# A two-layer graph network on one core: work reordered at both ends of the program

## The chip, the core and the metric

The kernel runs on one core of a Trainium2 chip. Five engines work side by side, each in the order of its own queue: TensorE (PE) multiplies matrices, VectorE (DVE), ScalarE (ACT) and GpSimd (POOL) work elementwise, and SyncE (SP) issues most of the transfers (DMAs). They wait for each other on semaphores. The metric is the time of one execution on the device, in microseconds (us); lower is better.

## The reference

There are 32 items of 512 nodes with 512 features, one 512 x 512 adjacency matrix, and two layers. The first is masked attention of 8 heads of 64 features, the second a graph convolution with a symmetrically normalized adjacency; each adds its input and normalizes.

```python
def _L0_gnn_ref(x, adj, Wq, bq, Wk, bk, Wv, bv):
    q = (x @ Wq + bq).reshape(b, n, H, HD)          # k, v likewise; H = 8, HD = 64
    scores = jnp.einsum('bihd,bjhd->bhij', q, k) / jnp.sqrt(jnp.float32(HD))
    scores = scores + jnp.where(adj == 0, -1e9, 0.0)[None, None, :, :]
    out = jnp.einsum('bhij,bjhd->bihd', jax.nn.softmax(scores, axis=-1), v)
    return out.reshape(b, n, H * HD)

def _L1_gnn_ref(x, adj, weight, bias):
    d = jnp.where(adj.sum(axis=1) > 0, jax.lax.rsqrt(adj.sum(axis=1)), 0.0)
    norm_adj = adj * d[:, None] * d[None, :]
    return jnp.einsum('nm,bmo->bno', norm_adj, jnp.einsum('bni,io->bno', x, weight)) + bias

x = _layernorm(x + _L0_gnn_ref(x, adj, Wq, bq, Wk, bk, Wv, bv))
x = _layernorm(x + _L1_gnn_ref(x, adj, weight, bias))
```

## The kernel before

**Order.** The program is written out by hand. Small helper functions return lists of pieces, a piece being one product and what follows it; `run`, `weave` and `cut` put the lists in an order, and the wrapper `InOrder` pins every engine to the order in which the program names its instructions. That wrapper records each instruction, so all of them show as line 44 in the profile, and they are told apart by their tiles. `unshifted` is the fast way through; it counts conditions under which its arithmetic is not good enough in `bad`, and `general` would run only if `bad` were positive.

**Products in seven parts.** The 512-wide products with the weights are made of seven half-size products instead of eight, so the operands need combinations: a tile of seven slots holds four quarters (0 to 3), and slots 4, 5, 6 and then 2 are made by subtracting or adding slots. `combine` does that for the transposed x (tile `XT`, in the profile xT), `weigh` for the weights `wv`, `wk`, `wq`, `w1`. `seven` yields the seven pieces k = 0 to 6 in the slot order (0,0), (1,1), (5,5), (6,6), (4,4), (3,2), (2,3). Each piece writes one PSUM tile of the pool `ps_mm`, which has three buffers (tile mm), and VectorE or ScalarE takes it from there into running sums e1, u2 and the results.

**Start.** The first x is not transposed by VectorE but turned by PE: `turn_first(j, i)` multiplies with the identity into an mm tile and copies that into XT[:, 2j+i], VectorE for i = 0, ScalarE for i = 1. In the queues, `weigh(wv)` and `weigh(wk)` stand on POOL, `values_of(0)` (value products; `middle` forms u2 and adds the value bias bv_r to it on POOL), then `keys_and_queries(0, 0)` and `(0, 1)` with the adjacency between them. `adjacency` writes the mask, and the adjacency twice: adjT in the rounded type that the convolution uses, and plainT unrounded. `compare(m)` later tests one quarter of the two for differences (a comparison that writes plainT and a reduction into `lost`).

**Middle.** `blocks` has four blocks of two heads for each item. In each block PE makes scores twice (pool ps_sc, two buffers, tile sc), VectorE clips and masks them (e<-sc,maskT), ScalarE exponentiates, POOL sums the exponentials (acc) and PE multiplies them with the values (av). Between these, `shares` deals out the products for the next item and the convolution of the one before. During item 0 the side work is a dictionary `beside`, keyed by the place of a piece in the list of products for item 1; all four `compare` stand behind pieces 10 and 12 there.

**End.** For item 31 (b = B - 1) there is nothing left to run beside. `finish` has `add_pair` (attention output and residual), `measure`, `root` (on POOL, the reciprocal root), `norm` (writes x1 and its rounded part HI, tile hi), `low` (the remainder, tile lo), `lift` (adds the layer's bias b1_r on POOL), `grow` and `judge` (three small checks on VectorE). `convolve` has `block(m)` (eight products with adjT into two sc tiles), `unload` and `parts` (the result into XT and its combinations), `second` (the seven products with w1), `extend` (POOL adds or subtracts), `measure`, `root` and `store`. For item 30, the pieces k = 4, 5, 6 of `second` are copied by ScalarE to tiles called side and summed by `extend(4)` to `extend(6)`. In the last lines `c` is the convolution of item 30 with its pieces `s`, `e` that of item 31, and `end` is `finish(31)`.

Of the kernel before, what the change touches and what calls it, by code (L numbers as in the profile page):

```python
# [17 lines left out]
P = 128  # L18
# [31 lines left out]
def unshifted(  # L50
# [29 lines left out]
    B, N, D = x.shape  # L80
# [4 lines left out]
    tensor, vector, scalar, gpsimd = (InOrder(tc, e) for e in (nc.tensor, nc.vector, nc.scalar, nc.gpsimd))  # L85
# [15 lines left out]
    HALF = N // 2  # L101
    X = {}
    XT = consts.tile([P, 7, 2, HALF], F32, name="xT")
# [14 lines left out]
    def turn(b, j):  # L118
# [4 lines left out]
        if j == 0 and b > 1:  # L123
            load_x(b, 1)

    def turn_first(j, i):

        p = ps_mm.tile([P, 2, HALF], F32, name="mm")
        for n in range(2):
            for u in range(2):  # L130
                for q in range(4):
                    at = q * P + (2 * i + u) * 32
                    tensor.matmul(
                        p[32 * q : 32 * (q + 1), u, ts(n, P)], R[0][2 * j + n][:, at : at + 32], ident,
                        start=True, stop=True,
                    )
        (scalar.copy if i else vector.tensor_copy)(XT[:, 2 * j + i], p)

    def combine(b, at):
        to, a, c = ((4, 2, 0), (5, 3, 4), (6, 3, 2), (2, 5, 1))[at]  # L140
        engine = gpsimd if b else vector
        engine.tensor_tensor(XT[:, to], XT[:, a], XT[:, c], ALU.subtract)
# [34 lines left out]
    def weigh(t, engine):  # L177
        for at in range(4):
            weigh_part(t, engine, at)
# [15 lines left out]
    for i in range(2):  # L195
# [3 lines left out]
        if i == 0:  # L199
            bv_r = load_row(bv, "bv_r", nc.scalar)  # L200
    wk = load_parts(Wk, "wk", nc.sync)
# [11 lines left out]
    b1_r = load_row(b1, "b1_r", nc.sync)  # L213
# [101 lines left out]
    def values_of(b):  # L315


        def multiply(p, i, j):
            for r in range(2):
                for u in range(2):  # L320
                    tensor.matmul(
                        p[:, r, :], XT[:, j, u, ts(r, P)], wv[:, i, u, :],
                        start=u == 0, stop=u == 1,
                    )

        def first(e1, p):
            V[b] = acts.tile([P, NT, D], F32, name="v")
            vector.tensor_add(e1, p, bv_r[:, None, :HALF].to_broadcast([P, 2, HALF]))

        def middle(u2, u1, p):  # L330
            vector.tensor_add(u2, u1, p)
            gpsimd.tensor_add(u2, u2, bv_r[:, None, HALF:].to_broadcast([P, 2, HALF]))

        def out(i, j):
            return V[b][:, 2 * j : 2 * j + 2, ts(i, HALF)]

        return seven(multiply, first, middle, out)
# [33 lines left out]
    E, ACC, AV, SM, YT, HI, LO = {}, {}, {}, {}, {}, {}, {}  # L371
# [126 lines left out]
    def finish(b):  # L498
# [96 lines left out]
            )  # L595

        def lift(i):
            gpsimd.tensor_add(YT[b][:, i, :], YT[b][:, i, :], b1_r)

        def grow(i):  # L600
            x1 = YT[b][:, i, :]
# [5 lines left out]
        def behind(f):  # L607
# [6 lines left out]
            pairs=[[(0, add_pair, (i, g)) for i in range(NT)] for g in ORDER],  # L614
            halves=[(0, root, (0, 2)), (0, root, (2, 2))],
# [156 lines left out]
    def run(pieces):  # L772
        for _, f, args in pieces:
            f(*args)
# [21 lines left out]
    put_off = [(0, more, ())]  # L796
# [2 lines left out]
    blocks = [(b, g) for b in range(B) for g in ORDER]  # L799
    S = len(blocks)  # L800
    weigh(wv, gpsimd)
    weigh(wk, gpsimd)
    first = values_of(0)
    turn_first(0, 0)
    turn_first(0, 1)
# [1 line left out]
    value_biases()  # L807
    turn_first(1, 0)
    turn_first(1, 1)
    combine(0, 0)  # L810
    combine(0, 1)
    run(first[1:2])
    combine(0, 2)
    combine(0, 3)
    scalar.activation(wq[:, :4], wq[:, :4], AF.Copy, scale=SCALE)
    run(first[2:])
    biases()
    wq_parts = [(0, weigh_part, (wq, vector, k)) for k in range(4)]
    first = keys_and_queries(0, 0)
# [6 lines left out]
    for k in range(S + 1):  # L826
        b, at = divmod(k, G)
        if at == 1:
            if 1 < b < B - 1:
                load_residual(b - 1)  # L830
            if b + 2 < B:
                load_x(b + 2, 0)
            if b + 1 < B:
                main, kq = keys_and_queries(b + 1, 0), keys_and_queries(b + 1, 1)
                if b:
                    main = values_of(b + 1) + main
                turn0, turn1 = turns(b + 2) if b + 2 < B else ([], [])
                main += kq[:5]
            if b == 0:
                w1_parts = [(0, weigh_part, (w1, gpsimd, i)) for i in range(4)]  # L840
                exact = [(0, compare, (m,)) for m in range(NT)]
                main += kq[5:]
                beside = {
                    2: put_off, 3: [(0, degrees, ())] + put_off, 6: put_off, 7: w1_parts[:1] + put_off,
                    8: w1_parts[1:2], 9: turn0 + w1_parts[2:3], 10: put_off + exact[:2], 11: put_off + w1_parts[3:],
                    12: exact[2:], 13: turn1,
                }
                side = early[5:6] + put_off + early[6:] + put_off
                side += sum(([piece] + beside.get(i, []) for i, piece in enumerate(main)), [])
                shares = cut(side, (4, 4, 4, 4))  # L850
            elif b < B - 1:
                f, c = finish(b - 1), convolve(b - 1)
                norm, low, grow, measure = f["norm"], f["low"], f["grow"], f["measure"]


                beside = {
                    0: rest[:1], 1: rest[1:3], 3: rest[3:4] + put_off, 4: rest[4:5],
                    5: rest[5:6] + f["inverse"] + put_off, 6: rest[6:] + f["scale"][:2], 7: f["scale"][2:] + f["add"],
                    8: measure[:2] + put_off, 9: measure[2:], 10: f["root"] + put_off, 11: norm[:1],
                    12: norm[1:2] + low[:1], 13: norm[2:3] + low[1:2], 14: norm[3:] + low[2:3],  # L860
                    15: low[3:] + f["lift"], 16: put_off + grow[:2], 17: put_off + grow[2:], 18: turn0 + f["judge"],
                }
                side = sum(([piece] + beside.get(i, []) for i, piece in enumerate(main)), [])
                side += c["first"] + c["parts"] + kq[5:] + turn1[:1]
                s = c["second"]
                if b < B - 2:
                    side += put_off + s[:1] + put_off + s[1:3] + turn1[1:2] + s[3:4] + turn1[2:3] + s[4:5]
                    side += turn1[3:4] + s[5:6] + c["measure"][:1] + turn1[4:] + s[6:] + c["measure"][1:2]
                    rest = c["measure"][2:] + c["root"] + c["store"]
                    shares = cut(side, (8, 8, 8, 8))  # L870
                else:
                    held, h, last = c, s, finish(b)
                    scale, add = last["scale"], last["add"]
                    side += h[:1] + last["inverse"] + h[1:2] + scale[:2] + h[2:3] + scale[2:] + add
                    shares = cut(side, (8, 8, 8, 4))
            else:
                f, c, last = last, convolve(b - 1), finish(b)
                s, first, low, lift, pairs = c["second"], c["first"], f["low"], f["lift"], last["pairs"]
                within = low[:1]
                shares = [  # L880
                    h[3:4] + f["measure"] + f["root"] + h[6:] + f["norm"] + f["judge"],
                    h[4:5] + low[1:3] + h[5:6] + low[3:] + lift + put_off + put_off + last["early"] + first[:2]
                    + held["measure"][:2] + first[2:3] + held["measure"][2:] + first[3:] + c["parts"] + f["grow"],
                    held["root"] + s[:2] + pairs[0] + pairs[1],
                    [],
                ]
# [40 lines left out]
    norm, low, lift, block, pairs, extend = end["norm"], end["low"], end["lift"], e["block"], end["pairs"], c["extend"]  # L927
    run(end["late"][:1] + pairs[2] + end["late"][1:] + s[2:3] + held["store"])
    run(sum((pairs[3][i : i + 1] + end["measure"][i : i + 1] for i in (0, 1)), []) + end["halves"][:1] + s[3:5])
    run(sum((pairs[3][i : i + 1] + end["measure"][i : i + 1] for i in (2, 3)), []) + extend[:1] + end["halves"][1:])  # L930
    run(s[5:6] + norm[:2] + low[:1] + block[:1] + low[1:2] + block[1:2] + lift[:1] + extend[1:2] + norm[2:] + low[2:3])
    run(block[2:3] + low[3:] + lift[1:2] + block[3:] + lift[2:] + end["judge"])

# [8 lines left out]
    vector.tensor_add(count, count, more)  # L944
    vector.memset(ones, 1.0)

    run(e["unload"] + e["parts"] + s[6:] + end["grow"] + extend[2:] + c["measure"][:2])
    s, tail, halves = e["second"], c["measure"][2:] + c["root"] + c["store"], e["halves"]
    run(s[:2] + halves[0] + s[2:3] + tail[:1] + s[3:4] + tail[1:3] + s[4:5])
    p = ps_mm.tile([1, 1], F32, name="mm")  # L950
    tensor.matmul(p, count, ones, start=True, stop=True)
    vector.tensor_scalar(bad, p, -1.0, float(P * B * NT * H + N), op0=ALU.mult, op1=ALU.add)
    run(tail[3:] + s[6:] + e["measure"][2:] + e["roots"][1:] + e["stores"][2:] + s[5:6] + halves[1] + e["roots"][:1])
    run(e["stores"][:2])
    return nc.values_load(bad, min_val=0, max_val=P * B * NT * H + N * N + N)

# [281 lines left out]
```

## Time and profile before

| | |
|---|---|
| time, median of 3 runs | 2820.21 us (2820.18 to 2822.76) |
| the profiled execution | 2821.64 us; span of the profile 2819.7 us |
| granted TensorE clock | 0.997 |
| TensorE busy | 2792.0 us, 99% of the span |
| VectorE, GpSimd, ScalarE busy | 2177.5, 1786.4, 1050.1 us |
| one POOL operation of two inputs, 128x512 | 1.28 us (yT<-yT,b_r, mean of 124) |
| one VectorE operation on PSUM and SBUF, 128x512 | 0.69 us (kq<-u,mm, mean of 128) |
| five value products (40 matmuls) in a row, from 16.07 | 8.87 us |

A profile is of one execution. Times of rows are from the span's start. Of a row "14.36 1.58" the first number is its start and the second its duration; consecutive rows of one engine overlap by about 0.1 us. A wait is idle time of an engine, put down to the instruction that ended it. The chain follows the last instruction back through what released it; "issue" in it is time for which the profile shows no releaser.

### The profile page before, as it was taken

To read this page: it belongs to the slowest core of one execution; us is meant where nothing else is said; L and a number is where in the kernel's file an instruction comes from. 1 tells how busy PE (TensorE), PEld (TensorE's weight loads), DVE (VectorE), ACT (ScalarE), POOL (GpSimd) and SP (SyncE) were. 2 spreads that over 40 slices of the span, in tenths; PEclk is the share of its full clock that TensorE was granted. 3 is DMA by queue.
4 is the path that set the end of the run, shared out by engine and by line. 5 is a ranking of instruction groups with operands and counts; after the bars stand their busy time and mean duration, and the time that the engine had idled before them with its cause. 6 is when DMAs were issued, how large, how long until landed. Compare 5 with 4: busy or idle time off the path is not lost.

```text
span 2819.7 us, 34592 instructions
## 1 busy us (share of the span) xinstructions
PE 2792.0 (99%) x12540; PEld 1874.8 (66%) x12540; DVE 2177.5 (77%) x3201; ACT 1050.1 (37%) x1323; POOL 1786.4 (63%) x1174
## 2 busy tenths in 40 slices
PE   8999999999999999999999999999999999999997
PEld 6566666666666666666666666666666666666655
DVE  5877877788777787777787778877777777778777
ACT  2333333343333433334333334333343333443343
POOL 3666665666666666666666666666666666666656
PEclk9999999999999999999999999999999999999999
DMA  4111121112221122221112211222112122112211
GB/s 120 32 29 49 49 59 43 43 48 52 57 57 42 38 52 54 57 45 42 49 49 60 53 42 37 53 56 57 42 41 53 49 56 46 42 49 49 60 38 50
DMA packets 379107, 141.04 MB, mean 50 GB/s; under 512 B 277808, under 2 KB 345392, under 8 KB 378928
## 3 DMA queue, kind: packets, MB, share of 16 engines
q1 hardware_dynamic: 377776, 137.17, 20.4%
q8 instruction: 101, 1.65, 0.2%
q10 hardware_dynamic: 1152, 1.57, 0.2%
q14 instruction: 78, 0.64, 0.1%
HBM read 71.83 MB, written 33.55 MB: 37 GB/s over the span
## 4 chain that ended last, share of the span: by engine, by line
PE 97%; DVE 2%; POOL 0%; issue 0%; DMA 0%; ACT 0%; POOLq 0%; DVEq 0%; ACTq 0%
PE mm L44 64%; PE sc L44 17%; PE av L44 16%; DVE e L44 1%; DVE xT L44 0%; DVE plainT L44 0%; POOL xT L44 0%; POOL acc L44 0%; DVE st L44 0%; DVE y L44 0%; DMA xr<-in_x_dram 0%; DVE lo L44 0%; DVE kq L44 0%; DVE lost L44 0%; DVE ve L44 0%
## 5 line engine op out<-in xcount | busy, mean ns | idle before, releaser
L44 ACT ACTIVATE e<-e 128x1024 f32<-128x1024 f32 x512 | 540.9, 1057 | 1075.8 <-DVE e L44 1059.2
L44 POOL TENSOR_TENSOR acc<-acc,e 128x1024 f32<-128x1024 f32 x248 | 587.5, 2369 | 94.3 <-ACT e L44 87.1
L44 DVE SCALAR_TENSOR_TENSOR e<-sc,maskT 128x1024 f32<-128x1024 f32 x512 | 597.9, 1208 | 22.1 <-PE sc L44 21.9
L44 PE MATMUL sc<-kq 64*128 64x512 f32 x2048 | 510.1, 616 | 3.6 <-DVE e L44 3.5
L44 PE MATMUL mm<-xT,wk 128*128 128x256 f32 x1792 | 469.7, 384 | 2.4 <-issue 2.0
L44 PE MATMUL av<-e,v 128*64 128x512 f32 x2048 | 467.9, 598 | 0.0
L44 PE MATMUL mm<-xT,wq 128*128 128x256 f32 x1792 | 459.9, 379 | 0.0
L44 PEld LDWEIGHTS mm<-xT,wk 128*128 128x128 f32 x1792 | 332.2, 190 | 115.9 <-issue 72.9
L44 PE MATMUL mm<-wv,xT 128*128 128x256 f32 x1792 | 405.3, 383 | 1.8 <-DVE xT L44 1.3
L44 PEld LDWEIGHTS mm<-wv,xT 128*128 128x128 f32 x1792 | 336.3, 191 | 72.7 <-issue 25.3
L44 POOL TENSOR_TENSOR acc<-e 128x1024 f32<-128x1024 f32 x126 | 297.2, 2359 | 134.3 <-ACT e L44 134.3
L44 PEld LDWEIGHTS mm<-xT,wq 128*128 128x128 f32 x1792 | 340.5, 190 | 46.3
L44 PEld LDWEIGHTS sc<-kq 64*128 64x128 f32 x2048 | 175.9, 186 | 271.4 <-issue 203.1
L44 PEld LDWEIGHTS av<-e,v 128*64 128x64 f32 x2048 | 135.5, 136 | 316.2 <-issue 293.4
L44 POOL TENSOR_TENSOR yT<-yT,b_r 128x512 f32<-128x512 f32 x124 | 154.6, 1279 | 167.7 <-DVE lo L44 167.7
L44 DVE TENSOR_TENSOR kq<-u,mm 128x512 f32<-128x512 f32 x128 | 88.0, 688 | 221.9 <-PE mm L44 221.6
L44 PE MATMUL mm<-w,zT 128*128 128x256 f32 x992 | 224.9, 379 | 0.7 <-ACT side L44 0.7
L44 POOL TENSOR_TENSOR rstd<-ve,minus_half 128x4 f32<-128x4 f32 (+1 forms) x66 | 66.1, 1001 | 234.1 <-DVE nmu L44 234.1
L44 PEld LDWEIGHTS mm<-w,zT 128*128 128x128 f32 x992 | 188.2, 190 | 28.1 <-issue 1.5
L44 PE MATMUL mm<-adjT,hi 128*128 128x512 f32 x496 | 202.1, 407 | 0.0
L44 POOL TENSOR_TENSOR yT<-yT,xr 128x512 f32<-128x512 f32 x124 | 154.4, 1278 | 73.6 <-DVE yT L44 73.6
L44 PE MATMUL mm<-adjT,lo 128*128 128x512 f32 x496 | 195.9, 395 | 0.5 <-DVE lo L44 0.5
(141 smaller groups left out, 3254.5 us busy)
## 6 DMA issues: line engine op xcount, KB each, us to landing
out_dram<-y SPq DMA_DIRECT2D x127, 256.0 KB, 2.1
x<-in_x_dram SPq DMA_DIRECT2D x248, 128.0 KB, 2.9
yT<-yb SPq DMA_DIRECT2D x496, 64.0 KB, 2.5
xr<-in_x_dram SPq DMA_DIRECT2D x122, 256.0 KB, 3.3
wk<-in_L_gnn_Wk_dram SPq DMA_DIRECT2D x8, 128.0 KB, 5.0
wq<-in_L_gnn_Wq_dram SPq DMA_DIRECT2D x8, 128.0 KB, 4.3
yT<-in_adj_dram SPq DMA_DIRECT2D x1, 1024.0 KB, 6.0
w<-in_L_gnn_weight_dram SPq DMA_DIRECT2D x2, 512.0 KB, 7.6
```

The source lines that it names most:

```text
L44: return self.tc.keep_in_program_order(op(*args, **kwargs))
```

## The change

- `turn_first`: for j = 1 the PSUM tile is no longer only copied. XT[:, 4] is formed by VectorE from the PSUM tile and XT[:, 0]; slot 2 is not copied at all (a later combination writes it). ScalarE still copies slot 3; XT[:, 5] and XT[:, 6] are formed from the two PSUM tiles. `combine(0, 0)` to `(0, 2)` go.
- `weigh(wk)` is named behind the fourth value piece instead of ahead of the first.
- The value bias is added on VectorE for items 0 and 1.
- The four comparisons stand behind product pieces 0, 5 and 7 of item 1's list, and the last behind the first value piece for item 2.
- At the end, norm(0) stands ahead of item 30's piece k = 5 and its copy; lift goes behind all of low, two of its four additions to VectorE, the order on POOL being lift(3), lift(2), extend(5), extend(4); judge and the counting move from ahead of unload to behind item 31's piece k = 2; the count's product goes behind k = 6.

```diff
@@ turn_first
-        (scalar.copy if i else vector.tensor_copy)(XT[:, 2 * j + i], p)
+        if j == 0:
+            (scalar.copy if i else vector.tensor_copy)(XT[:, i], p)
+        elif i == 0:
+            turned["B12"] = p
+            vector.tensor_sub(XT[:, 4], p, XT[:, 0])
+        else:
+            scalar.copy(XT[:, 3], p)
+            vector.tensor_sub(XT[:, 5], p, XT[:, 4])
+            vector.tensor_sub(XT[:, 6], XT[:, 3], turned["B12"])
@@ values_of, middle
-            gpsimd.tensor_add(u2, u2, bv_r[:, None, HALF:].to_broadcast([P, 2, HALF]))
+            engine = gpsimd if b > 1 else vector
+            engine.tensor_add(u2, u2, bv_r[:, None, HALF:].to_broadcast([P, 2, HALF]))
@@ finish, lift
-            gpsimd.tensor_add(YT[b][:, i, :], YT[b][:, i, :], b1_r)
+            engine = vector if b == B - 1 and i < 2 else gpsimd
+            engine.tensor_add(YT[b][:, i, :], YT[b][:, i, :], b1_r)
@@ start
     weigh(wv, gpsimd)
-    weigh(wk, gpsimd)
     first = values_of(0)
...
-    combine(0, 0)
-    combine(0, 1)
     run(first[1:2])
-    combine(0, 2)
     combine(0, 3)
     scalar.activation(wq[:, :4], wq[:, :4], AF.Copy, scale=SCALE)
-    run(first[2:])
+    run(first[2:4])
+    weigh(wk, gpsimd)
+    run(first[4:])
@@ item 0
-                    2: put_off, 3: [(0, degrees, ())] + put_off, 6: put_off, 7: w1_parts[:1] + put_off,
-                    8: w1_parts[1:2], 9: turn0 + w1_parts[2:3], 10: put_off + exact[:2], 11: put_off + w1_parts[3:],
-                    12: exact[2:], 13: turn1,
+                    0: exact[:1], 2: put_off, 3: [(0, degrees, ())] + put_off, 5: exact[1:2], 6: put_off,
+                    7: w1_parts[:1] + put_off + exact[2:3], 8: w1_parts[1:2], 9: turn0 + w1_parts[2:3], 10: put_off,
+                    11: put_off + w1_parts[3:], 13: turn1,
                 }
+                rest = exact[3:]
@@ end
-    run(sum((pairs[3][i : i + 1] + end["measure"][i : i + 1] for i in (2, 3)), []) + extend[:1] + end["halves"][1:])
-    run(s[5:6] + norm[:2] + low[:1] + block[:1] + low[1:2] + block[1:2] + lift[:1] + extend[1:2] + norm[2:] + low[2:3])
-    run(block[2:3] + low[3:] + lift[1:2] + block[3:] + lift[2:] + end["judge"])
+    run(sum((pairs[3][i : i + 1] + end["measure"][i : i + 1] for i in (2, 3)), []) + end["halves"][1:])
+    run(norm[:1] + s[5:6] + low[:1] + norm[1:2] + block[:1] + low[1:2] + block[1:2] + norm[2:] + low[2:3])
+    run(block[2:3] + low[3:] + block[3:] + lift[3:] + lift[:3] + extend[1:2] + extend[:1])
+    run(e["unload"] + e["parts"] + s[6:] + end["grow"] + extend[2:] + c["measure"][:2])
+    s, tail, halves = e["second"], c["measure"][2:] + c["root"] + c["store"], e["halves"]
+    run(s[:2] + halves[0] + s[2:3] + end["judge"])
...
-    run(e["unload"] + e["parts"] + s[6:] + end["grow"] + extend[2:] + c["measure"][:2])
-    s, tail, halves = e["second"], c["measure"][2:] + c["root"] + c["store"], e["halves"]
-    run(s[:2] + halves[0] + s[2:3] + tail[:1] + s[3:4] + tail[1:3] + s[4:5])
+    run(s[3:4] + tail[:1] + s[4:5] + tail[1:3] + s[6:])
     p = ps_mm.tile([1, 1], F32, name="mm")
     tensor.matmul(p, count, ones, start=True, stop=True)
...
-    run(tail[3:] + s[6:] + e["measure"][2:] + e["roots"][1:] + e["stores"][2:] + s[5:6] + halves[1] + e["roots"][:1])
+    run(tail[3:] + e["measure"][2:] + e["roots"][1:] + e["stores"][2:] + s[5:6] + halves[1] + e["roots"][:1])
```

More of the change, by code (lines that the diff above doesn't have):

```diff
@@ L124, in turn @@
             load_x(b, 1)
+    turned = {}
     def turn_first(j, i):
```

## The prediction

> **What bounds the kernel now.** I read the busy times first, then what TensorE (PE) waited for, then the chain of waits at both ends, then the timelines of VectorE (DVE) and GpSimd (POOL) around each wait. PE is busy 99% of the span and 97% of the chain, so only PE's waits can be won, plus the stretch after its last product. Columns of a wait: total us, times, longest.
>
> ```profile
> PE 2792.0 (99%) x12540; PEld 1874.8 (66%) x12540; DVE 2177.5 (77%) x3201; ACT 1050.1 (37%) x1323; POOL 1786.4 (63%) x1174
> ```
> ```profile
> PE sc L44 <- DVE e L44: 3.5, 2, 3.3
> PE sc L44 <- ACT hi L44: 2.2, 1, 2.2
> PE mm L44 <- issue: 2.0, 1, 2.0
> PE mm L44 <- DVE xT L44: 1.3, 1, 1.3
> ```
>
> All four lie at the ends: 1.3 at 14.8 and 2.0 at 24.96 (first value products), 3.3 at 131.2 (end of item 0's attention), 2.2 at 2782.1 (last graph convolution). Between 140 and 2700 us PE never waits, so I leave that stretch as it is. The rows behind the waits (start, us, engine):
>
> ```profile
> 121.41 2.29 DVE L44 TENSOR_TENSOR plainT<-plainT,adjT 128x512 f32<-128x512 f32 x1
> 123.73 0.69 DVE L44 TENSOR_REDUCE lost<-plainT 128x1 f32<-128x512 f32 x1
> ...
> 128.88 0.69 DVE L44 TENSOR_TENSOR plainT<-plainT,adjT 128x512 f32<-128x512 f32 x1
> ```
> ```profile
> 98.78 2.35 DVE L44 SCALAR_TENSOR_TENSOR e<-sc,maskT 128x1024 f32<-128x1024 f32 x2
> ```
> ```profile
> 98.63 2.38 POOL L44 TENSOR_TENSOR acc<-acc,e 128x1024 f32<-128x1024 f32 x1
> ```
> ```profile
> 2790.84 1.26 DVE L44 TENSOR_SCALAR low<-inv 128x32 f32<-128x32 f32 x1
> 2792.14 1.23 DVE L44 SCALAR_TENSOR_TENSOR low<-inv,low 128x32 f32<-128x32 f32 x1
> 2793.40 0.19 DVE L44 TENSOR_REDUCE fine<-low 128x1 f32<-128x32 f32 x1
> ```
> ```profile
> 2788.63 4.69 POOL L44 TENSOR_TENSOR wv<-wv,b_r 128x512 f32<-128x512 f32 x3
> ```
>
> See that one comparison takes 2.29 or 0.69, and that tiny checks of 32 columns take 1.26 while POOL works beside them.
>
> **What the Trainium skill says.** "SBUF — State Buffer", Who interferes with whom: VectorE with two SBUF inputs, or in a two-port mode (tensor_scalar may enter one), and a GpSimd instruction that reads SBUF exclude each other for a whole instruction; tensor_reduce never contends. The trace agrees: the 2.29 comparison began inside a POOL accumulation (120.79), the 0.69 one with POOL idle; the checks above waited out one 1.26 us POOL addition each, the reduce (0.19) none. "TensorE: Matmul & The Clock Gate", What's actually happening: after an idle window of some 3.4 us the array runs at half clock until it has been busy about as long. Here, after the 3.3 wait, the 8 score and 66 other matmuls took 2.82 + 15.42; the same counts at 2647.89 took 1.92 + 14.34, so 2.0 was lost on top. The 1.3 and 2.0 waits of the start left no such trace.
>
> **Head: combinations of x out of PSUM.** Before, VectorE copied XT[:,2] (0.69 from 12.09), then formed XT[:,4] and XT[:,5] from SBUF (1.44, 1.57, in turn with POOL's wv combinations), done at 15.93. Now XT[:,4] is one PSUM subtraction at 12.09, priced at 0.69 (the row e<-mm,bv_r, one PSUM and one SBUF input); XT[:,5] follows when the second turning ends (12.9), done at 13.65; XT[:,6] waits for ScalarE's copy of XT[:,3] (13.55), done at 14.3, which also frees the bank it holds before the product that needs it. Late next is wv[:,5] on POOL: it started at 13.79 and no longer shares, so 1.27, done at 15.05. The third value product starts at 15.15 instead of 16.07: **0.9**.
>
> **Head: value bias of item 0.** PE's 2.0 at 24.96 is a bank of ps_mm (three): the first key product needs the bank of value product k=4, whose readers stand behind v<-u, which waited for u<-u,bv_r on POOL (24.28, behind four wk combinations from 18.70). On VectorE it follows u at 19.4: 0.68, plus at most one wk combination (1.27) waited out, so by 21.4; two readers later (1.2) the bank is free by 22.6; PE's seventh product ends at 15.15 + 5 x 1.73 = 23.8 (five took 8.87 from 16.07). No wait: **2.2** (2.0 and the gap to a normal step). Next to be late is scaled wq (ScalarE until 24.45), needed at 24.66. Together 3.1; bounds 2.2 (wv or wq late) and 3.3. Moving weigh(wk) behind two more pieces moves nothing: in the built queues POOL's four wk combinations still follow those of wv, as the bias behind them is gone. Loads don't eat it: the adjacency lands at 19.34 + 6.0 and is first used at 40.85 - 3.1; DMA is silent from 35 to 50 us.
>
> **Value bias of item 1.** v<-u waited 4.08 for POOL until 70.35, and the scores at 72.83 started 0.13 late and took 2.26 instead of 1.99. Now the addition waits for POOL's accumulation (until 66.7) and ends at 67.3, 3 us ahead: **0.4** (0 to 0.5). POOL's accumulations move up by 1.27; nobody waits for them.
>
> **Comparisons.** Four pairs (121.41 to 127.09, 128.88 to 131.53) are 8.3 us of VectorE ahead of the score operation at 133.28. Without them it starts when its scores are there (about 128), 131.2 is met, and 3.3 + 2.0 = 5.3 goes. What each costs in its new place:
> - Pair 0 behind v at 79.69: POOL accumulates until 81.7, so done by 82.9; the 1.94 idle before 82.30 covers all but 0.6, and the next score operation (83.30) starts 0.2 late, with 1 us of idle at 91-93 to recover.
> - Pair 1 ahead of the score operation at 98.78: POOL's accumulation (98.63) is first by 0.15. The comparison ends at 101.01 + 0.6, the reduce at 102.2, the two score operations at 103.35 and 104.5. PE's next scores (102.14) need those two banks: 1.3 + 0.15 = **1.45 lost**. If VectorE wins the race, 0; if the halved clock follows, 3.4.
> - Pair 2 behind kq at 106.33: VectorE is 3.5 late by pair 1 and waits for an accumulation again (until about 112.2), done at 113.4. The scores then at 112.6 use banks read by 109.8; those at 118.1 need a score operation that ends at 117: covered, by 1.1.
> - Pair 3 among item 2's value products, where VectorE idled 0.65 + 1.04 + 1.04 + 1.38 us: covered; at most 2.9 is added.
>
> Net **3.85**; bounds 1.9 and 5.3.
>
> **Tail.** Here k counts the seven products of second, first of item 30 (its sums are c's), then of item 31. norm(0) goes ahead of item 30's side copy: its rstd is there at 2780.6, so hi is written by 2782.25 instead of 2784.28, just as PE ends product k=5 (2782.1). extend(4) and the lifts leave the time of norm and low: norm(1) and norm(3) took 1.5 each and low 1.7 each beside POOL's additions, 0.55 and 0.69 alone. Then low(3) ends at 2788.65 (2790.92 before); PE still waits some 1.5 for hi(1) and low(0), and ends its 32 products at 2791.35 instead of 2793.44: 2.1 gained, as the half clock there (4 products in 1.9 instead of 1.1) goes too.
>
> It doesn't last. On VectorE two lifts (0.6 each, with one POOL lift of 1.25 between) run to 2791.1, unload, combinations (in turn with the four additions now waiting on POOL) and c's measure to 2796.5-2797.7, and item 31's product k=2 is taken by 2799.5-2800.2, 2.2-2.9 ahead. There judge and the counting now stand, 3.55 us as before: POOL is at extend(6) and (2) back to back, so low, low and the first count each wait out an addition. Before, only 0.95 of this lay behind PE's products; here all of it does. k=3 is taken at 2803.1-2803.7 (2803.17 before), the root waits for extend(3), k=6 is taken at 2806.5-2807.1 (2806.19 before), and bad adds 0.13 behind it. The remaining chain (6.4 to the last normalization at 2812.59) is unchanged. I take **+0.5**; bounds -2.1 (no waits for POOL: PE's gain reaches the end) and +1.5. The matmul of the count moves behind k=6, 0.1 us.
>
> **Sum.** -3.1 - 0.4 - 3.85 + 0.5 = -6.85 against the profiled execution (2821.64, span 2819.7 and 1.9 around it). That is 1.4 above the median of the runs; the difference carries over to the median: 2820.2 - 6.85 = 2813.4.
>
> **Rivals.**
> - The tail keeps PE's gain (checks find POOL idle): -2.1 instead of +0.5, -9.45, 2810.8. For it: the counts took 0.16 with POOL idle; against: POOL has ten additions in a row from 2788.7. 0.20.
> - Pair 1 halves the clock (+1.95) and the tail is at its late alignment (+1.0): -4.4, 2815.8. For it: 2.19 us of wait with 0.73 shortly before did halve it at 2784; against: 1.3 and 2.0 at the start did not. 0.27.
> - The change does less than it says: wq or wv land later and hide the head's 3.1: -3.75, 2816.5. 0.05.
> - Slower: a pair costs VectorE up to 2.9 us, and the blocks it goes to have less idle (1.94, none, 2.61). If lateness isn't recovered, each of the three repeats the stall of 131.2, 3 x 5.3 = 15.9 against 5.3 removed: -6.85 + 15.9 - 1.45 = +7.6, 2827.8. It decides once a score operation ends over 2 us after PE wants its bank; I count 1.3 at the worst. 0.04.
>
> **Numbers.** My case has 0.44. A measurement of this kernel can tell about 0.2% (5.6 us) from no change: faster is my case and the first rival, 0.64; within it, the second and third, 0.32; slower 0.04. The range 2810.2 to 2817.6 holds all but the last case and the outer ends of the bounds.
>
> **What would show it.** Right: PE's waits of 2.0 and 3.3 gone, key products from 23.8, one new wait of some 1.4 near 100 us, in the tail PE's 32 block products over about 2 us sooner while item 31's k=6 is taken no sooner, and judge's low at about 1.2 each after k=2. Wrong: a second half-clock stretch near 100 us, a wait at 83 or 112, or a last normalization over 1.5 us from its old distance to item 30's product k=5.

## The result, and the profile after

| | before | changed |
|---|---|---|
| time, median | 2821.66 us (9 runs) | 2813.65 us (9 runs, 2812.72 to 2813.97) |
| ratio | | 0.9971, interval 0.9961 to 0.9982 |
| profiled execution (span) | 2821.64 (2819.7) | 2813.97 (2812.1) |

The change takes 7.7 us off the profiled execution and 8.0 off the median. The interval leaves out 1, so the gain is there, though it is 0.3% of the time. The busy times of the page after hardly differ from those of before, as they should where the order changes and the work hardly does:

```profile
PE 2788.9 (99%) x12540; PEld 1872.9 (67%) x12540; DVE 2176.4 (77%) x3204; ACT 1049.7 (37%) x1323; POOL 1781.0 (63%) x1170
```

The news is in TensorE's waits (total us, times, longest), here those of the changed kernel:

```profile
PE sc L44 <- DVE e L44: 1.5, 2, 1.2
PE mm L44 <- DVE y L44: 1.1, 1, 1.1
PE mm L44 <- ACT side L44: 0.7, 1, 0.7
```

Of the four waits of before, those of 3.3, 2.2 (for hi) and 2.0 are gone, and that of 1.3 at the third value product has become 0.4. Two new ones stand there: 1.2 for VectorE's score operation, which lies at 100 us, and 1.1 for y, ahead of the last product (2797.24). Waits alone don't tell where a gain is kept, though. For that I number TensorE's matmuls from 0 in the order in which they start and compare the start of the same number in two traces. Number 144 begins the third value product, 184 the first key product, 400 lies in item 0's attention at about 72 us, 12,400 shortly ahead of the last convolution. Six stretches then cover nearly the whole span, and runs of one kernel agree to a few hundredths in most of them. Each is a distance in us, between two starts or between a start and the end that is named:

| kernel | first wv combination on POOL to 144 | 144 to 184 | 184 to 400 | 400 to 12,400 | 12,400 to end of last normalization | from there to end of span |
|---|---|---|---|---|---|---|
| before | 3.63 | 10.89 | 48.05 | 2697.24 | 41.14 | 6.28 |
| changed | 2.67 | 8.74 | 47.91 | 2693.52 | 40.30 | 6.50 |
| comparisons back | 2.68 | 8.74 | 47.78 | 2697.22 | 40.30 | 5.38 |
| bias on GpSimd | 2.67 | 8.74 | 47.98 | 2693.52 | 40.29 | 6.18 |
| bias on GpSimd, wk back | 2.68 | 10.88 | 48.06 | 2693.54 | 40.28 | 6.45 |
| accumulation ahead of degrees | 2.67 | 8.74 | 47.57 | 2691.96 | 40.28 | 6.28 |
| combinations back | 3.40 | 8.74 | 47.58 | 2693.53 | 40.31 | 5.99 |
| end back | 2.67 | 8.74 | 47.96 | 2693.52 | 41.17 | 5.46 |
| checks in a gap | 2.67 | 8.74 | 47.97 | 2693.54 | 38.84 | 6.30 |
| both of these | 2.68 | 8.74 | 47.58 | 2691.94 | 38.83 | 6.44 |
| changed, second run | 2.68 | 8.74 | 47.58 | 2693.58 | 40.30 | 6.57 |
| combinations back, second run | 3.63 | 8.71 | 47.59 | 2693.56 | 40.30 | 6.31 |
| end back, second run | 2.67 | 8.74 | 48.29 | 2693.57 | 41.14 | 5.57 |

See that an edit shows in one or two columns and leaves the others alone, and that the last column varies for other reasons as well (5.38 to 6.57). What stands ahead of the first column is the landing of wv, which moved the start of POOL's first combination between 11.80 and 13.20 us from one profile to the next. It was 12.44 both before and in the changed kernel's first profile. The third column varies with the landing of wq: with the bias on VectorE it is 47.57 to 47.59 in the five profiles in which TensorE didn't wait for scaled wq, and 47.78 to 48.29 in the five in which it did. This is why single spans of these kernels can't be compared below about 1 us.

Head of the changed kernel: VectorE's timeline (start, us) first, then GpSimd's, and below that GpSimd's bias addition in the kernel before.

```profile
13.46 0.69 DVE L44 TENSOR_TENSOR xT<-mm,xT 128x512 f32<-128x512 f32 x1 [0.80 <-ACT xT L44]
14.06 0.68 DVE L44 TENSOR_TENSOR xT<-xT,mm 128x512 f32<-128x512 f32 x1
14.73 0.69 DVE L44 TENSOR_TENSOR v<-e,mm 128x512 f32<-128x512 f32 x1
...
19.59 1.68 DVE L44 TENSOR_TENSOR u<-u,bv_r 128x512 f32<-128x512 f32 x1
```

```profile
12.44 5.52 POOL L44 TENSOR_TENSOR wv<-wv 128x512 f32<-128x512 f32 x4 [10.15 <-DMA wv<-in_L_gnn_Wv_dram]
18.12 5.64 POOL L44 TENSOR_TENSOR wk<-wk 128x512 f32<-128x512 f32 x4 [0.16 <-DMA wq<-in_L_gnn_Wq_dram]
```

```profile
24.28 1.26 POOL L44 TENSOR_TENSOR u<-u,bv_r 128x512 f32<-128x512 f32 x1
```

The combinations from PSUM take 0.69 and 0.68 where the SBUF ones, beside POOL's combinations of wv, took 1.44 and 1.57. The bias addition has two SBUF inputs, and 1.68 is what it takes if it waits out the rest of one wk combination ahead of its own 0.68. It starts at 19.59, where POOL's started at 24.28. The chain of waits shows what is late next:

```profile
18.81 3.97 DMA wq<-in_L_gnn_Wq_dram
...
22.96 1.92 ACT wq L44
24.88 0.04 issue
24.93 7.17 PE mm L44 x32
```

Pair 1 near 100 us, again VectorE and then GpSimd:

```profile
95.51 2.75 DVE L44 TENSOR_TENSOR plainT<-plainT,adjT 128x512 f32<-128x512 f32 x1
98.30 0.69 DVE L44 TENSOR_REDUCE lost<-plainT 128x1 f32<-128x512 f32 x1
98.90 2.35 DVE L44 SCALAR_TENSOR_TENSOR e<-sc,maskT 128x1024 f32<-128x1024 f32 x2
```

```profile
95.37 2.35 POOL L44 TENSOR_TENSOR acc<-acc,e 128x1024 f32<-128x1024 f32 x1
```

POOL's accumulation is first by 0.14, the comparison needs 2.75 instead of 0.68, and the score operation behind it starts at 98.90. The other pairs took 1.39, 2.55 and 0.68 for the comparison, and no wait of TensorE follows them. The checks after item 31's k = 2 on VectorE, and GpSimd beside them:

```profile
2791.69 0.67 DVE L44 TENSOR_TENSOR e<-e,mm 128x512 f32<-128x512 f32 x1
2792.28 0.58 DVE L44 TENSOR_SCALAR low<-inv 128x32 f32<-128x32 f32 x1
2792.89 1.20 DVE L44 SCALAR_TENSOR_TENSOR low<-inv,low 128x32 f32<-128x32 f32 x1
...
2795.10 0.68 DVE L44 TENSOR_TENSOR u<-e,mm 128x512 f32<-128x512 f32 x1
```

```profile
2790.31 2.50 POOL L44 TENSOR_TENSOR y<-y,side 128x512 f32<-128x512 f32 x2
2792.77 1.26 POOL L44 TENSOR_TENSOR y<-wv,e 128x512 f32<-128x512 f32 x1
2795.86 1.26 POOL L44 TENSOR_TENSOR y<-wv,u 128x512 f32<-128x512 f32 x1 [1.82 <-DVE u L44]
```

VectorE takes item 31's k = 2 and k = 6 in the kernel before at

```profile
2801.76 0.67 DVE L44 TENSOR_TENSOR e<-e,mm 128x512 f32<-128x512 f32 x1
...
2806.19 1.28 DVE L44 TENSOR_TENSOR y<-y,mm 128x512 f32<-128x512 f32 x2 [0.26 <-PE mm L44]
```

and k = 6 in the changed kernel at

```profile
2798.36 1.27 DVE L44 TENSOR_TENSOR y<-y,mm 128x512 f32<-128x512 f32 x2
```

### The profile page after: what moved, and what is told of

It is laid out like the page before. It is cut to its first block, busy times and chain, and to the rows that moved or that the text cites. A ratio compares the mean times of both kernels' runs of the same rounds, so it can differ in the third digit from the quotient of the medians.

```text
span 2812.1 us, 34592 instructions
## 1 busy us (share of the span) xinstructions
PE 2788.9 (99%) x12540; PEld 1872.9 (67%) x12540; DVE 2176.4 (77%) x3204; ACT 1049.7 (37%) x1323; POOL 1781.0 (63%) x1170
## 3 DMA queue, kind: packets, MB, share of 16 engines
q10 hardware_dynamic: 1152, 1.57, 0.2%
## 4 chain that ended last, share of the span: by engine, by line
PE 97%; DVE 2%; DMA 1%; issue 0%; ACT 0%; POOL 0%; ACTq 0%; SPq 0%; POOLq 0%; DVEq 0%
PE mm L44 63%; PE sc L44 17%; PE av L44 16%; DMA wv<-in_L_gnn_Wv_dram 0%; DVE st L44 0%; DVE e L44 0%; DVE y L44 0%; DVE xT L44 0%; DMA bk_c<-in_L_gnn_bk_dram 0%; DMA wq<-in_L_gnn_Wq_dram 0%; DVE lo L44 0%; DVE mv L44 0%; DVE plainT L44 0%; POOL xT L44 0%; DVE ve L44 0%
```

## The experiments

Each undoes or alters one thing in the changed kernel; the diffs are against it. The first four ran beside each other and beside 36 runs of the kernel before (median 2821.49), the next four beside 24 (2821.01), the last three beside 19 (2821.84).

### Comparisons back in one place

```diff
-                    0: exact[:1], 2: put_off, 3: [(0, degrees, ())] + put_off, 5: exact[1:2], 6: put_off,
-                    7: w1_parts[:1] + put_off + exact[2:3], 8: w1_parts[1:2], 9: turn0 + w1_parts[2:3], 10: put_off,
-                    11: put_off + w1_parts[3:], 13: turn1,
+                    2: put_off, 3: [(0, degrees, ())] + put_off, 6: put_off, 7: w1_parts[:1] + put_off,
+                    8: w1_parts[1:2], 9: turn0 + w1_parts[2:3], 10: put_off + exact[:2], 11: put_off + w1_parts[3:],
+                    12: exact[2:], 13: turn1,
...
-                rest = exact[3:]
```

> The changed kernel with its four comparisons back behind pieces 10 and 12 of item 1's list; all else as changed. Theory: the change won 5.1 us at the end of item 0's attention (wait and half clock) and lost 1.36 near 100 us to pair 1, so this kernel takes 3.8 us longer than the changed one (span about 2815.9), the wait near 100 us is gone and PE again waits some 3.3 us for the score operation near 131. Rival: the score operation was late mainly because the head and item 1's bias ran later, so with those mended the comparisons in their old place cost under 1 us.

Measured: 2817.1 us, 0.9984 of before (0.9976 to 0.9991). Its waits of TensorE:

```profile
PE sc L44 <- DVE e L44: 3.5, 2, 3.3
```

The stall of 131 is back, the wait at 100 is gone, and only the fourth column moves: 2697.22, which is the 2697.24 of before and 3.70 more than the changed kernel. The theory had 3.8, so it holds, and the rival's "under 1 us" falls. The span came to 2813.9 and not to the 2815.9 of the theory because wv landed 0.64 earlier here and the last column is 1.1 shorter. This is the largest single part, a gain of 5.26 (between matmuls 600 and 700) less the 1.56 lost at pair 1.

### Value bias on GpSimd again, and then wk back as well

```diff
-            engine = gpsimd if b > 1 else vector
+            engine = gpsimd
```

> The changed kernel with the value bias of items 0 and 1 back on GpSimd, the wk combinations still behind the fourth value piece. Theory (the wait at 24.96 came from the bias standing behind four wk combinations): on GpSimd the bias now comes ahead of wk, is done at about 20.8, and the head stays where it is, within 0.3 us; item 1 loses 0.3; span 2812.1 to 2812.7. Rival (it has to be on VectorE): the key products start 2 us later, span about 2814.4.

Measured: 2813.87 us, 0.9972 (0.9961 to 0.9982), so nothing that the medians can tell. Between value products and key products 8.74 stays 8.74. Item 1's part shows in the third column: 47.98, with no wait for scaled wq, against 47.58, so 0.40 (0.48 in the next experiment). In the queue of POOL the bias now comes ahead of wk:

```profile
20.39 1.27 POOL L44 TENSOR_TENSOR u<-u,bv_r 128x512 f32<-128x512 f32 x1 [1.56 <-DMA wq<-in_L_gnn_Wq_dram]
21.62 5.20 POOL L44 TENSOR_TENSOR wk<-wk 128x512 f32<-128x512 f32 x4
```

The second edit of this pair puts `weigh(wk, gpsimd)` ahead of the first value piece, where it was:

```diff
+    weigh(wk, gpsimd)
     first = values_of(0)
...
-    run(first[2:4])
-    weigh(wk, gpsimd)
-    run(first[4:])
+    run(first[2:])
```

> The changed kernel with the value bias of items 0 and 1 back on GpSimd and the wk combinations back ahead of the value pieces. Theory: the wait of about 2 us ahead of the first key product returns (bias at about 23.8 behind wk), the start of the key products moves from 23.85 to about 25.9; with item 1's 0.3 the span is about 2814.2 (the scaled wq hid 0.2 of it). Rival: the scaled wq, there at 24.9, is what holds the head, and the return of the wait costs under 1 us.

Measured: 2816.32 us, 0.9981 (0.9974 to 0.9989), 2.45 over the kernel with only the bias put back. TensorE's wait and POOL's queue:

```profile
PE mm L44 <- issue: 2.0, 1, 2.0
```

```profile
18.65 5.19 POOL L44 TENSOR_TENSOR wk<-wk 128x512 f32<-128x512 f32 x4
23.80 1.27 POOL L44 TENSOR_TENSOR u<-u,bv_r 128x512 f32<-128x512 f32 x1
```

The bias stands behind four wk combinations again and starts 3.4 us later; 10.88 is the 10.89 of before. So wk behind the bias is a cure that is enough by itself. The bias on VectorE alone was not run. In the changed kernel POOL's queue at the head is four wv and then four wk combinations with nothing between them, so with the bias on VectorE it makes no difference to POOL where wk is named; that this is a second cure is argued from the queue, not measured.

### Accumulation ahead of the degrees

POOL's accumulation at 95.37 stood behind two small degree operations (the second at 94.39, 1.01). Put in front of them (`put_off` holds the accumulation), it runs at once:

```diff
-                    0: exact[:1], 2: put_off, 3: [(0, degrees, ())] + put_off, 5: exact[1:2], 6: put_off,
+                    0: exact[:1], 2: put_off, 3: put_off + [(0, degrees, ())], 5: exact[1:2], 6: put_off,
```

> The changed kernel with one swap in item 1's list: the put-off accumulation stands ahead of the degrees instead of behind them, so that on GpSimd it comes ahead of the two powers. Theory (pair 1 waits out the accumulation that starts 0.14 us before it, both reading SBUF): the accumulation runs at about 90.4 to 92.8, the comparison takes 0.7 instead of 2.75, PE's wait near 100 us goes, 1.4 us less, span about 2810.7. Rival (pair 1 is slow or late for another reason, the VectorE queue is simply full there): the wait stays at 0.8 or more and the span within 0.6 of 2812.1.

Measured: 2812.44 us, 0.9967 (0.9954 to 0.9979). VectorE near 96 us in this kernel:

```profile
95.48 0.68 DVE L44 TENSOR_TENSOR plainT<-plainT,adjT 128x512 f32<-128x512 f32 x1
96.20 0.69 DVE L44 TENSOR_REDUCE lost<-plainT 128x1 f32<-128x512 f32 x1
96.80 2.34 DVE L44 SCALAR_TENSOR_TENSOR e<-sc,maskT 128x1024 f32<-128x1024 f32 x2
```

The comparison takes 0.68, the wait at 100 is gone, and the fourth column falls by 1.56. That pair 1 lost its 1.56 to this one accumulation is shown.

### Combinations of x back

```diff
-        if j == 0:
-            (scalar.copy if i else vector.tensor_copy)(XT[:, i], p)
-        elif i == 0:
...
+        (scalar.copy if i else vector.tensor_copy)(XT[:, 2 * j + i], p)
...
+    combine(0, 0)
+    combine(0, 1)
     run(first[1:2])
+    combine(0, 2)
```

> The changed kernel with the combinations of the first x formed from SBUF again, as before; all else as changed. Theory: the third value product starts 0.8 to 1.2 us later behind the wv combinations (XT[:,5] at about 15.9, and POOL slowed by VectorE's reads), and nearly all of it reaches the key products, as the bias no longer hides it: span 0.7 to 1.0 above the changed kernel. Rival: the scaled wq holds the second half of the first key product anyway, so under 0.3.

Measured: 2813.88 us, 0.9975 (0.9966 to 0.9984), and in the second run, beside the changed kernel itself (2814.05, 0.9973, 0.9963 to 0.9983):

> The changed kernel itself, on one chip with the next two, so that parts worth under 1 us can be set against it. Expected at 0.9971 of the kernel before, within 0.0005.

> The combinations of x back as copies and SBUF operations, beside the changed kernel of the same call. Measured from the start of POOL's first combination of wv, the third value product should come at 3.40 us instead of 2.67, as in the earlier run of this edit. Theory: 0.73 us is lost where scaled wq is early, less where PE has to wait for wq anyway: 0.3 to 0.7 us slower than the changed kernel. Rival: scaled wq hides all of it, under 0.2 us.

2814.24 us, 0.9973 (0.9963 to 0.9983). In the traces the third value product comes 3.40 and 3.63 us behind POOL's first combination of wv, not 2.67, so the 0.7 to 1.0 is real there. In the medians 0.2 is left, which these runs can't tell from none, so they decide neither for the 0.3 to 0.7 of the theory nor for the rival. Part of it can be hidden by scaled wq: in the changed kernel's first profile TensorE waited for that until 24.93, in the second (24.24) it did not. Of the eight profiles that have the changed head, five show such a wait, worth 0.20 to 0.71 in the third column, and the mean over the eight is 0.25; the two with the combinations back show none (47.58 and 47.59). So wq hides some of the gain, but by these profiles not all of it.

### The order of the end back

The edit restores `lift` on POOL and all lines of the end as they were in the kernel before; it is the last part of the diff above, reversed.

> The changed kernel with the end in its old order (side copy ahead of norm(0), lifts on POOL and early, checks and counting ahead of unload); all else as changed. Theory: PE's wait of 2.2 ahead of the last convolution returns and its 32 products end 2.7 later, but VectorE gets the checks' place back, so only 0.85 is lost from the last attention products to the last normalization (41.15 us again instead of 40.3). Rival (the end's reordering brings nothing, as predicted): within 0.3 or faster by up to 0.5.

Measured: 2813.8 us, 0.9975 (0.9967 to 0.9984). As the trace said 0.87 and the median next to nothing, it ran again beside the changed kernel:

> The order of the end as it was, beside the changed kernel of the same call. Theory, from the trace of the earlier run of this edit (41.17 us from one of the last matmuls before the end to the last normalization, against 40.30): 0.9 us slower than the changed kernel. Rival: the medians of the earlier call, which leave 0.2 us or less: the last transfers take back what the engines lose.

2814.19 us, 0.9972 (0.9961 to 0.9983), against 2814.05. The rival holds: on the engines the old order costs 0.84 to 0.87 (fifth column), and behind the last normalization it gets that back (sixth: 5.46 and 5.57, against 6.50 and 6.57 in the two profiles of the changed kernel; over all eight with the changed end 5.38 to 6.57, mean 6.21). The stores differ. Here the third and the last store that SP issues, and ScalarE's last normalization, in the changed kernel (three views of short stretches):

```profile
2802.06 1.36 SPq L765 DMA_DIRECT2D out_dram<-y  x1
```

```profile
2806.22 0.34 SPq L765 DMA_DIRECT2D out_dram<-y  x1
```

```profile
2804.75 0.81 ACT L44 ACTIVATE y<-y,add,rstd 128x512 f32<-128x512 f32 x1 [0.58 <-POOL add L44]
```

and the same with the end back (second run):

```profile
2803.25 0.33 SPq L764 DMA_DIRECT2D out_dram<-y  x1
```

```profile
2806.70 0.33 SPq L764 DMA_DIRECT2D out_dram<-y  x1
```

```profile
2805.87 0.81 ACT L44 ACTIVATE y<-y,add,rstd 128x512 f32<-128x512 f32 x1 [0.56 <-POOL add L44]
```

With the end back the last store is issued 0.03 us after the last normalization ends (2806.68), in the changed kernel 0.65 after (2805.57). Two things on SP lie before it. One of the stores takes 1.36 us to issue instead of 0.33. And SP reads `bad` from memory, which takes 0.86 at 2804.94, 0.63 ahead of the end of the last normalization, with the last store queued behind; with the end back that read takes 0.50 and comes 2.37 ahead, behind the fourth store. The kernel before read it at the same place, yet its last store was at 0.28, one of its stores having taken 1.16 to issue. Over the eight profiles that have the changed end untouched, the last store was issued 0.12 to 0.73 after the last normalization and the span ended 5.26 to 5.86 after that issue.

That the stretch behind the last normalization takes the gain back is what the fifth and the sixth column show for these four profiles, and the medians agree (2814.05 and 2814.19). That the late last store does it is not shown. With the checks in a gap (next experiment) SP reads `bad` earlier, 1.87 ahead of the end of the last normalization, and issues the last store later, 1.31 behind it, one store having taken 1.54; yet the sixth column is 6.30. And there is a rival. In the changed kernel's profile the transfers nearly stop from 2803.0 to 2804.0 (12 and 61 GB/s in the two halves), about where the long issue ends, and then run at 340 to 393 GB/s until 2808.0. So the DMA engines were busy for some 1.5 us after the last store had been issued, and an earlier issue may have gained nothing. With the end back (second run) the near-stop is some 0.5 us (16 GB/s from 2805.5 to 2806.0), around the end of an issue of 0.53. No run changes the one without the other, and why an issue takes 1.36 in one profile and 0.33 in another is open.

### The checks in a gap of VectorE

Between norm(1) and low(1) POOL is idle and TensorE has block products to do. `judge` and the counting go there:

```diff
-    run(norm[:1] + s[5:6] + low[:1] + norm[1:2] + block[:1] + low[1:2] + block[1:2] + norm[2:] + low[2:3])
+    run(norm[:1] + s[5:6] + low[:1] + norm[1:2] + end["judge"])
...
+    run(block[:1] + low[1:2] + block[1:2] + norm[2:] + low[2:3])
...
-    run(s[:2] + halves[0] + s[2:3] + end["judge"])
+    run(s[:2] + halves[0] + s[2:3])
```

> The changed kernel with judge and the counting moved between norm(1) and low(1) of item 31, where VectorE idles 0.8 us and POOL has nothing to add. Theory (the checks cost 2.8 us on the chain because they stand there alone and wait out POOL's additions): they take about 1.3 in the gap, 0.5 of it late for PE, and the stretch between the products k=2 and k=3 loses 2.8; until PE's k=6 binds again 1.3 to 1.8 us are won. Rival (POOL's ten additions bind the end, not the checks): under 0.5 is won.

Measured: 2812.53 us, 0.9970 (0.9958 to 0.9982). VectorE:

```profile
2776.69 0.17 DVE L44 TENSOR_SCALAR low<-inv 128x32 f32<-128x32 f32 x1
2776.89 0.20 DVE L44 SCALAR_TENSOR_TENSOR low<-inv,low 128x32 f32<-128x32 f32 x1
```

With POOL idle the two take 0.17 and 0.20 instead of 0.58 and 1.20; the whole group of checks fits in 1.5 us (2776.69 to 2778.17), and the fifth column falls by 1.46. The wait of 1.1 for y ahead of the last product is gone too.

### Both

> The changed kernel with both the accumulation ahead of the degrees and the checks in the gap. Theory: the two gains are at different ends and add: 1.35 and 1.3 to 1.8, together 2.7 to 3.1 below the changed kernel, about 2810.8 by the median. Rival: the gains overlap, under 2 us together.

The last edit and the accumulation ahead of the degrees together: 2810.41 us, 0.9962 (0.9949 to 0.9976), 10.6 us under the 2821.01 beside it. It keeps both gains (2691.94 and 38.83) and is the fastest version here.

## Why the prediction was right, and where its terms were off

The forecast was -6.85 us on the profiled execution; it was -7.67, of which 7.61 lies within the span. Stretch by stretch, from the starts of matmuls 400, 600, 700 and 12,400 in the two traces:

| stretch | predicted | measured |
|---|---|---|
| up to 400 (head and item 1's value bias) | -3.1 - 0.4 | -3.27 |
| 400 to 600 (pairs 0 to 2) | +1.45 | +1.57 |
| 600 to 700 (stall of 131) | -5.3 | -5.25 |
| 700 to 12,400 | 0 | -0.04 |
| to the end of the last normalization | +0.5 | -0.84 |
| from there to the end of the span | 0 | +0.22 |

**Head.** The third value product was to start at 15.15, and started at 15.11; key products were to start at 23.8, and started at 23.85. That these starts were met took equal landings of wv in the two profiles, which is chance; the distances of the first two columns (0.96 and 2.15 less, together the 3.1 of the forecast) don't depend on that. One step was off without harm: XT[:,5] was to follow the second turning at 12.9, but its row started at 13.46, put down to ScalarE's copy, and wv[:,5] was late enough to cover it. Scaled wq was named as late next, and TensorE waited for it until 24.93. It hid 0.33 (47.91 against the 47.58 of the second run). Without that, item 1's value bias won 0.40 to 0.48, where 0.4 was forecast. "Moving weigh(wk) behind two more pieces moves nothing" holds only because the bias moved as well: that move alone removes the 2.0, as the second experiment shows. The prediction gave the 2.2 to the bias, and didn't see that the other move brings it by itself.

**Comparisons.** What was to be lost at pair 1 (1.45) and won at 131 (5.3) came to 1.56 and 5.26 when tried alone, and the reason given, an accumulation first by 0.15, was the reason. The rival that the wait halves the clock fell: the wait was 1.2, and the eight score products behind it took 2.26 us, as against 3.01 behind the wait of 3.3 in the first experiment; the granted clock was 1.00 from 100 to 103 us, and 0.50 from 132 to 135 in that experiment. The rule on who excludes whom, from the Trainium skill, "SBUF — State Buffer", Who interferes with whom, carried all these numbers: 2.75 or 0.68 for one comparison, 1.20 or 0.20 for one check, depending on whether POOL was in an addition.

**The end.** This is the mis-sized term: +0.5 was forecast, -0.84 measured to the last normalization. To compare the traces, 6.99 is taken off the times of before, the distance of their matmuls 12,400. TensorE ended its 32 products 2.66 sooner, where 2.1 was forecast: its one wait there, for lo, was 0.43, where some 1.5 was forecast. Item 31's k = 2 was taken 3.08 sooner, where the prediction had 2.2 to 2.9. The checks then were to take 3.55, as before: low, low and the first count each waiting out an addition. They took 2.82. POOL's row at 2792.77 is the last addition that was ready; the next, at 2795.86, waited for u itself, which stands behind the checks. So there was nothing left for the counts to wait for, and the first low met an addition that was half done (0.58). Ten additions in a row were counted on POOL, and the last of them depend on what VectorE does after the checks. So k = 3 was taken 1.08 sooner, 0.24 of it was lost on the way to k = 6, and k = 6 was taken 0.84 sooner rather than 0.3 to 0.9 later. This carried through. The sign named for a right forecast, k = 6 no sooner and each low at about 1.2, did not come. The first rival, that all of TensorE's gain is kept, is no better: more than half of the 2.66 was given back.

**What was left out.** The prediction kept the stretch behind the last normalization as it was. SP's queue was not followed there: the read of `bad`, later than before, stands among the last stores. The profile pair shows little of a loss there (+0.22); the profiled execution of before had one long issue itself, 1.16. The experiment shows 0.9 to 1.1 in its profiles, about the gain on the engines, so the end's new order is worth nothing that the medians can tell (2814.05 and 2814.19). Against that, +0.5 was near by luck, for reasons that were not the forecast's.

**The time.** The gain of the medians, 8.0, is 1.2 more than the forecast's 6.85. The time forecast, 2813.4, lies nearer to 2813.65 than that, since the runs of before beside it had a median of 2821.66 and not the 2820.21 that was reckoned from. That closeness is chance.

## What to carry to other kernels

Where two engines exclude each other, ask of each small operation that is moved not what it takes but what the other engine is doing at that moment: the same two checks cost 1.8 us in one place and 0.4 in another, and a queue swap on the other engine can be worth as much as moving the operation. When a gain shows on the engines and not in the median, follow the queue that issues the last stores, and the transfers behind it. And compare traces by the starts of the same matmuls: parts of 0.3 us stand out there which the variation of loads and stores, about 1 us, hides in the times.

## What the runs showed that was not expected

- The granted clock isn't settled by the lengths of the waits. Waits of 0.73 and 2.19 ahead of the last block products had halved it in the kernel before (the first eight products took 3.18 us from start to start, at a granted clock of 0.50 from 2785 to 2788). With the end back, waits of 0.73 and 2.2 stand at the same place, and the same eight products took 1.96 and 1.97 in the two runs, at 1.00. The Trainium skill, "TensorE: Matmul & The Clock Gate", What's actually happening, says that the gate looks at activity in windows of 3.4 us that run freely. How much of two waits falls into one window then depends on where the window lies, which would fit; the traces show the granted clock, not the windows, so this stays a reading. The wait of 3.26 at 131 us halved the clock in both profiles that have it, the single waits of 1.2 to 2.0 in none. Both 3.26 and 2.19 are shorter than the 3.4 us that the page gives for an idle window, so in this case a window that isn't idle throughout was enough.
- To issue one 256 KB store at the end took SP from 0.33 to 1.54 us, and the same store 0.33 in one profile of the kernel with the combinations back and 1.17 in the other. Around the end of such a long issue the core's transfers nearly stopped: 12 GB/s from 2803.0 to 2803.5 in the changed kernel (issue of 1.36), where 340 to 393 GB/s followed from 2804.0 on, and 8 GB/s from 2812.5 to 2813.0 in the kernel before (1.16). Which of the two causes the other, the traces don't show.
